# A mamba recurrence on one core: the order of three small matmul pieces around the D groups

## The chip, the cores and the metric

The kernel runs on one core of one Trainium2 chip. The metric is the device time of one execution in microseconds (us); smaller is better. Five engines work side by side, each through its own list of instructions in order, and wait for each other through semaphores: TensorE (PE, matmuls and transposes, into PSUM), VectorE (DVE), ScalarE (ACT), GpSimd (POOL) and SyncE (SP, which here issues the DMA transfers).

## What is computed

The reference chains four layers over an image tensor `x` of 4 x 64 x 128 x 128 in float32: a mamba block (layer 0), a windowed transform with a small block MLP (layer 1), two 3x3 convolutions with a pooled channel gate (layer 2), and a block with two convolutions, a mamba and a feed-forward part (layer 3). The change touches the two mambas only. Cut to what matters, a mamba computes, over tokens `t` of a sequence, with 128 inner channels and N states (16 in layer 0, 64 in layer 3):

```python
xc    = silu(conv4(u @ in_proj_x) + conv_b)        # causal, 4 taps
z     = u @ in_proj_z
dt, Bm, Cm = split(xc @ x_proj_w.T)
delta = softplus(dt @ dt_proj_w.T + dt_proj_b)
def step(h, t):
    h = h * exp(delta[t][:, None] * A) + (delta[t] * xc[t])[:, None] * Bm[t][None, :]
    return h, h @ Cm[t]
y = ys + xc * D
y = y * silu(z)
```

After it come an output projection and a normalization.

## The kernel before

Both mambas are one class, `_Mamba`. The 65536 tokens are cut into 64 chunks of TC = 1024. The recurrence of one chunk is done for 128 x N pairs of channel and state. Four states times 32 channels fill the 128 partitions, so one **group** (four states) takes ND = 4 **iterations**, one for each quarter j of the channels. One iteration is one scan over 1024 tokens on DVE (L593, `tensor_tensor_scan`), written into a ring of eight slots, and one product with C on POOL (L596). A chunk has 4 groups in layer 0 (16 iterations) and 16 in layer 3 (64). An iteration's place in its chunk is called its **position** here.

Groups come in two kinds; layer 0 has "DADA", layer 3 "DADAADAADADAADAA". They differ in how the scan's input, delta * xc * B, comes about:

- **A group**: ScalarE (L387, and one block in eight on POOL, L391) scales the transposed delta * xc by B into `bxT`; PE turns it back, eight 128x128 transposes an iteration (L494), into a PSUM tile `bx`. This PSUM tile is "tile i" of iteration i.
- **D group**: PE spreads B over the partitions once for the group (L500, two matmuls into a `bx` buffer), and DVE multiplies it by the loaded delta * xc in each iteration (L587) into another `bx` buffer.

There are two `bx` buffers. A D group holds both for its four iterations. So the transposes for the first tile of the A group behind it wait for the last L587 of the D group, and those for the second tile wait for the D group's last scan.

The output y of a chunk gathers in one PSUM buffer. `_sums(u, None)` opens it: eight matmuls of xc with a diagonal of D (L410). `_sums(u, h)` adds a group's four products, for half h of the tokens: four matmuls (L413), two and three iterations after the group's last. When a chunk's last group is in, `gated` multiplies y by silu(z) on DVE (L619, called at position 3 of the next chunk), and that frees the PSUM buffer for the next `_sums(u, None)`.

Everything else (projections, convolution, the small matmuls for delta, B and C, the output projection and its norm) is written as generators, called feeds. Each is cut into **pieces**: a few matmuls into the one PSUM buffer `pm`, which then is read by another engine before the next piece can have it. `ahead` makes xc and sz (pieces z and conv), `prepare` the recurrence's inputs (v, C, u, step, B, duT; u is not a piece but one DVE and one POOL instruction), `behind` the output (project, norm). They are put between the iterations in two ways:

- In layer 0 `slots` gives the iteration, counted from the start of the feed's own chunk, at which each piece goes in. With 16 iterations a chunk, -43 is position 5, -37 is 11, -24 is 8, -22 is 10, -21 is 11, -16 is 0, -14 is 2, -7 is 9. The budget there is 12 steps an iteration, more than is ever used.
- In layer 3 there are no slots. A `budget` says how many steps (one or a few matmuls) may go in beside each iteration: in an A group 0, in a D group 2, 2, 2, 1. A feed that waits gives a number of iterations to let pass.

The order of all this is written out by hand in `run`, and `pin` ties it down on every engine. One iteration i issues, in this order: the end of a finished piece; loads of C; the exponentials for the scan three ahead (ACT, L556); the scalings for the next A group; `behind` with `gated`, when a chunk is full; `produced(i + 1)`, which is the next tile's transposes or the next D group's spread; in a D group L587; the scan; the product with C; the state's copy after the fourth; sums that are owed; and, by `beside`, the pieces. `_sums(u, None)` is owed at the iteration of its group's last scan, so before the change it is issued behind that scan.

Of the kernel before, what the change touches and what calls it, by code (L numbers as in the profile page):

```python
# [12 lines left out]
ALU = mybir.AluOpType  # L13
# [5 lines left out]
B, C, HH, WW = 4, 64, 128, 128  # L19
HW = HH * WW  # L20
TC = 1024
NH = TC // 512
# [3 lines left out]
ND = DI // DD  # L26
# [117 lines left out]
class _Mamba:  # L144
# [173 lines left out]
    def prepare(self, c):  # L318
        nc, K, nst, xc = self.nc, self.K, self.nst, c["xc"]

        pos, e, l, u = (self.tmp(k) for k in ("pos", "e", "l", "u"))
# [4 lines left out]
        nc.scalar.activation(e, e, AF.Exp, scale=-1.0)  # L326
        nc.scalar.activation(l, e, AF.Ln, bias=1.0)

        yield self.slot(c, "C")
        r = self.wC.shape[1]  # L330
        pm = yield from self.piece(
# [4 lines left out]
        c["C"] = self.dram.tile([nst, TC], F32, name="c2", tag="c2")  # L336
        for h in range(NH):
            nc.sync.dma_start(c["C"][:, _COLS[h]], cr[r * h : r * h + nst, :512])

        yield self.slot(c, "u")  # L340
        nc.vector.tensor_scalar(u, e, 1.0, 1.0, ALU.add, ALU.subtract)
        nc.gpsimd.tensor_sub(u, e, u)
        yield self.slot(c, "step", 4)
        pm = yield from self.halves((K.eye, pos), (K.eye, l), (K.eye, u))
        nc.scalar.copy(pos, pm)
# [18 lines left out]
        duT = c["duT"] = self.wp.tile([P, NB, DI], F32, name="duT", tag="duT")  # L364
# [56 lines left out]
    def run(self, chunks, ahead, behind, leads, budget):  # L421
# [3 lines left out]
        nc = self.nc  # L425
        its, us = [], []
        for i, c in enumerate(chunks):
            c["no"] = i
            for g, kind in enumerate(self.kinds):
                u = {"c": c, "g": g, "kind": kind, "hc": [], "at": len(its), "last": len(its) + ND - 1}  # L430
# [18 lines left out]
        owed, full = [], None  # L449
# [35 lines left out]
        def produced(i):  # L485

            if i == n:
                return
            v, j = its[i]
            if v["kind"] == "A" or i == v["at"]:  # L490
                bx = bxs[i] = self.bp.tile([P, TC], F32, name="bx", tag="bx", bufs=2)
            if v["kind"] == "A":
                for k in range(NB):
                    nc.tensor.transpose(  # L494
                        bx[:, P * k : P * (k + 1)], v["bxT"][:, k, :, :, j].rearrange("p q e -> p (q e)"), self.K.eye
                    )
            elif i == v["at"]:
                v["B"] = bx
                for k in _COLS:
                    nc.tensor.matmul(bx[:, k], self.spread[v["g"]], v["c"]["xc"][:, k], start=True, stop=True)  # L500
# [25 lines left out]
        at = -1  # L526
        for c in chunks[1:]:
            at = max(at + 1, per * c["no"] - leads[0])
# [3 lines left out]
        for i, (u, j) in enumerate(its):  # L532
# [20 lines left out]
            while nexp < min(n, i + 4) and its[nexp][1] in its[nexp][0]["c"].get("dl", ()):  # L553
                v, k = its[nexp]
# [11 lines left out]
            while credit >= 0.5:  # L566
                if not todo:
# [4 lines left out]
                    v = groups[nmul]  # L572
# [6 lines left out]
            if full and full[0] <= i:  # L579
                started(behind(full[1], self.gated(full[1])), i)  # L580
                full = None
            produced(i + 1)
            if u["kind"] == "D":
                if i == u["at"]:
# [12 lines left out]
            if j == ND - 1:  # L597
                nc.gpsimd.tensor_copy(self.state[:, :, u["g"]], self.ring[:, slot - j : slot + 1, GAP + TC - 1])
            u["hc"].append(hc)
            if i == u["last"]:  # L600
                owed += [(i, u, None)] * (u["g"] == 0) + [(i + 2, u, h) for h in range(NH)]
            while owed and not full and (owed[0][0] <= i or i + 1 == n):
                _, v, h = owed.pop(0)
                self._sums(v, h)
                if v["g"] == self.ng - 1 and h == NH - 1:
                    full = i + 1, v["c"]
# [38 lines left out]
@with_exitstack  # L645
def layer0(ctx, tc, K, w, x, x1):
    nc = tc.nc
    slots = {"z": -43, "conv": -37, "v": -24, "C": -22, "u": -21, "step": -16, "B": -14, "duT": -7}
    slots |= {"project": 22, "rstd": 23, "store": 29}
    m = _Mamba(ctx, tc, K, 16, w, "DADA", {"xc": 3, "sz": 4, "tmp": 5}, slots)  # L650
    cp, wp = m.cp, m.wp
# [626 lines left out]
def layer3_mamba(ctx, tc, K, w, t3, x3, s3, n3):  # L1278

    nc = tc.nc  # L1280
# [74 lines left out]
            nc.sync.dma_start(_halves(n3[b], t0)[h], o[64 * h : 64 * (h + 1)])  # L1355

    chunks = [{"at": (b, t0), "reset": t0 == 0} for b in range(B) for t0 in range(0, HW, TC)]
    m.run(chunks, ahead, behind, (64, 36), [x for k in m.kinds for x in ([2, 2, 2, 1] if k == "D" else [0] * ND)])


@with_exitstack
# [265 lines left out]
```

## Time and profile before

| what | value |
|---|---|
| median of 3 runs | 19720.83 us (19693.8 to 19727.24) |
| profiled execution | 19736.35 us, span of its instructions 19734.5 us |
| mean granted TensorE clock in it | 0.869 |
| layer 0, first to last scan | about 71 to 3665 us |
| layers 1, 2 and the convolutions of 3 | about 3665 to 6226 us |
| layer 3's mamba, first to last scan | 6226 to 18439 us |
| layer 3's feed-forward part | 18439 us to the end |
| L593, the scan | x4848 at 2335 ns and x272 (the first of a sequence) at 2276 ns |
| L587, the product of a D group | x2048 at 1228 ns |
| L596, the product with C on POOL | x5120 at 2378 ns |
| L494, one transpose | x24576, mean 338 ns as recorded |
| L410, the D matmuls | x2048 records (two for each matmul), 592 to 1063 ns |

The page is one profiled execution. Its first part gives each engine's busy time, the second cuts the span into 40 slices and gives the busy share of each engine in tenths. Waits name the engine and line that stood still, and the instruction whose end released it. In the timeline a row is a start, a duration (of the whole row when several instructions are merged), engine, line, operation, output and inputs; what stands in brackets is the idle time of that engine before the row, and who ended it. Matmuls in float32 appear as two records, overlap each other, and their ends are modelled.

### The profile page before, as it was taken

How to read it: one execution, taken by the hardware profiler on the slowest of the kernel's cores; microseconds unless marked ns; L12 is line 12 of the kernel's file. 1: busy time of each engine (PE TensorE's matmuls, PEld its weight loads, DVE VectorE, ACT ScalarE, POOL GpSimd, SP SyncE). 2: the span in 40 equal slices, each digit the busy share in tenths (PEclk: the TensorE clock that was granted, in tenths of full speed). 3: DMA queues.
4: the chain of work that ended last, by engine and by line, in shares of the span. 5: the costliest groups of instructions: out<-in, count | busy, mean ns of one | idle time of the engine just before them, and what ended most of it. 6: DMA issues, size and time to landing. Idle time of an engine off the chain costs nothing. (4 is left out here: it accounts for less than half of the span.)

```text
span 19734.5 us, 238606 instructions
## 1 busy us (share of the span) xinstructions
PE 15294.8 (78%) x80186; PEld 7627.5 (39%) x80186; DVE 15836.0 (80%) x8739; ACT 14933.8 (76%) x30369; POOL 14205.9 (72%) x8094
## 2 busy tenths in 40 slices
PE   7778788778897777777777777777777777777777
PEld 3333333367434333333333333333333333333222
DVE  7888888722124999999999999999999999999755
ACT  7888888411324988889888888988889888888422
POOL 6888888500003898899988989998898988989300
PEclk8999899879998888888888888888888888888888
DMA  5555555300212232332323233232322323233111
GB/s 138 152 150 153 154 150 151 95 37 26 75 56 65 75 88 77 84 82 79 87 75 87 78 83 86 76 88 77 83 82 79 87 76 86 78 82 85 46 43 38
DMA packets 669524, 1722.89 MB, mean 87 GB/s; under 512 B 196785, under 2 KB 231937, under 8 KB 660865
## 3 DMA queue, kind: packets, MB, share of 16 engines
q1 hardware_dynamic: 668288, 1707.62, 31.6%
q8 instruction: 629, 10.31, 0.2%
q14 instruction: 607, 4.96, 0.1%
HBM read 1434.27 MB, written 272.63 MB: 86 GB/s over the span
## 5 line engine op out<-in xcount | busy, mean ns | idle before, releaser
L596 POOL TENSOR_TENSOR ring<-ring,cb 128x1024 f32<-128x1024 f32 x5120 | 12086.1, 2378 | 1653.5 <-DVE ring L593 1340.8
L593 DVE TENSOR_TENSOR_SCAN ring<-da,state,bx 128x1024 f32<-128x1024 f32 x4848 | 11143.4, 2335 | 971.1 <-PE bx L494 697.9
L556 ACT ACTIVATE da<-dl,A 128x1024 f32<-128x1024 f32 x5120 | 5868.2, 1146 | 1383.0 <-DVE ring L593 1365.9
L387 ACT ACTIVATE bxT<-duT,BT 128x128 f32<-128x128 f32 x21504 | 6757.2, 387 | 0.0
L494 PE MATMUL bx<-cst,bxT 128*128 128x128 f32 x24576 | 4458.7, 338 | 2842.8 <-DVE bx L587 2053.0
L494 PEld LDWEIGHTS bx<-cst,bxT 128*128 128x128 f32 x24576 | 3743.1, 214 | 4917.0 <-DVE bx L587 2068.7
L413 PE MATMUL y<-ring,cst 128*32 128x512 f32 x20480 | 3566.6, 660 | 332.4 <-POOL ring L596 332.2
L587 DVE TENSOR_TENSOR bx<-du,bx 128x1024 f32<-128x1024 f32 x2048 | 2515.5, 1228 | 339.6 <-PE bx L500 219.1
L413 PEld LDWEIGHTS y<-ring,cst 128*32 128x32 f32 x20480 | 532.3, 112 | 1735.7 <-POOL ring L596 856.1
L1145 PE MATMUL cv<-img,cw 64*64 64x512 f32 x9216 | 1008.2, 594 | 74.6 <-DMA img<-d_x 45.6
L500 PE MATMUL bx<-xc,spread 128*128 128x512 f32 x2048 | 1018.0, 620 | 1.4
L1427 POOL MEMSET h<- 128x18 f32 x64 | 8.3, 132 | 1180.5 <-PE pd L1489 793.5
L1076 POOL TENSOR_TENSOR xs<-xs,cl 128x1024 f32<-128x1024 f32 x32 | 74.9, 2340 | 1068.4 <-DVE cl L1075 1068.4
L391 POOL TENSOR_TENSOR bxT<-duT,BT 128x512 f32<-128x512 f32 x768 | 809.2, 1054 | 11.5 <-ACT duT L370 11.5
L1310 POOL MEMSET X<- 64x1 f32 x4 | 0.4, 89 | 1122.4 <-DMA cw<-in_l_conv_wT 1122.4
L1489 PE MATMUL pd<-h,diag 64*64 64x512 f32 x4608 | 687.9, 610 | 0.7 <-issue 0.7
L1145 PEld LDWEIGHTS cv<-img,cw 64*64 64x64 f32 x9216 | 437.2, 134 | 643.5 <-issue 568.0
L593 DVE TENSOR_TENSOR_SCAN ring<-da,bx 128x1024 f32<-128x1024 f32 x272 | 609.4, 2276 | 72.4 <-PE bx L494 52.8
L500 PEld LDWEIGHTS bx<-xc,spread 128*128 128x128 f32 x2048 | 347.7, 189 | 687.7 <-issue 464.1
L1461 DVE SCALAR_TENSOR_TENSOR g<-h,dww,g 128x2048 f32<-128x2048 f32 x256 | 602.0, 2352 | 11.2
L1441 ACT ACTIVATE h<-ph,ff_fc_b 128x384 f32<-128x384 f32 (+1 forms) x384 | 200.7, 577 | 497.9 <-PE ph L1436 480.1
L1059 ACT COPY O<-p 128x1024 f32<-128x1024 f32 x32 | 32.4, 1012 | 691.7 <-PE p L1052 691.7
(321 smaller groups left out, 13361.0 us busy)
## 6 DMA issues: line engine op xcount, KB each, us to landing
cb<-c SPq DMA_DIRECT2D x5120, 128.0 KB, 2.8
dl<-d SPq DMA_DIRECT2D x2048, 128.0 KB, 3.4
du<-d SPq DMA_DIRECT2D x2048, 128.0 KB, 3.0
d<-pos SPq DMA_DIRECT2D x128, 512.0 KB, 2.6
d<-u SPq DMA_DIRECT2D x128, 512.0 KB, 3.0
X<-d_t SPq DMA_DIRECT2D x124, 256.0 KB, 4.0
S<-in_x SPq DMA_DIRECT2D x120, 256.5 KB, 4.4
res<-in_x SPq DMA_DIRECT2D x128, 128.0 KB, 3.8
```

Source lines behind the costliest of these rows:

```text
L387: nc.scalar.activation(t[:, k, q].rearrange("p e j -> p (e j)"), c["duT"][:, k, :], AF.Copy, scale=c["BT"][:, k, n : n + 1])
L391: nc.gpsimd.tensor_mul(t[:, k].rearrange("p q e j -> p q (e j)"), c["duT"][:, k].unsqueeze(1).to_broadcast(shape), c["BT"][:, k, NQ * g : ...
L413: nc.tensor.matmul(c["y"][DD * j : DD * (j + 1), _COLS[h]], K.sel, hc[:, _COLS[h]], start=False, stop=u["g"] == self.ng - 1,)
L494: nc.tensor.transpose(bx[:, P * k : P * (k + 1)], v["bxT"][:, k, :, :, j].rearrange("p q e -> p (q e)"), self.K.eye)
L500: nc.tensor.matmul(bx[:, k], self.spread[v["g"]], v["c"]["xc"][:, k], start=True, stop=True)
L556: nc.scalar.activation(das[nexp], v["c"]["dl"][k], AF.Exp, scale=self.A[:, k, v["g"] : v["g"] + 1])
L587: nc.vector.tensor_mul(bxs[i], u["c"]["du"][j], u["B"])
L593: nc.vector.tensor_tensor_scan(hs, das.pop(i), bxs.pop(i), 0.0 if u["c"].get("reset") else st, ALU.mult, ALU.add)
L596: nc.gpsimd.tensor_mul(hc, hs, u["cb"])
L1145: nc.tensor.matmul(p[i][half[h]], W[half[i], k, :], src[half[i], at : at + 4, dx : dx + WW], start=k == 0, stop=k == 8,)
L1461: nc.vector.scalar_tensor_tensor(g1, tap, wk, g1, ALU.mult, ALU.add)
L1489: nc.tensor.matmul(pd[i][half[h]], diag[half[i], k, :], h0[half[i], r : r + 4, dx : dx + WW], start=k == 0, stop=k == 8,)
```

## The change

Four edits, in the two mambas:

1. `_sums(u, None)` of a chunk is owed from the first iteration of its first group, and is issued in the iteration of that group's last scan ahead of `produced(i + 1)`, so ahead of the first transposed tile behind this D group, and ahead of the last L587 and scan, where it stood behind them.
2. In layer 3 the budget beside the last iteration of a D group goes from 1 to 0.
3. In layer 0 the slots change: conv -37 to -38, C -22 to -18, u -21 to -22.
4. u's two instructions stand ahead of piece C in `prepare`, in both mambas.

```diff
@@ prepare
+        yield self.slot(c, "u")
+        nc.vector.tensor_scalar(u, e, 1.0, 1.0, ALU.add, ALU.subtract)
+        nc.gpsimd.tensor_sub(u, e, u)
+
         yield self.slot(c, "C")
...
-        yield self.slot(c, "u")
-        nc.vector.tensor_scalar(u, e, 1.0, 1.0, ALU.add, ALU.subtract)
-        nc.gpsimd.tensor_sub(u, e, u)
         yield self.slot(c, "step", 4)
@@ run
+            if not full and owed and owed[0][2] is None and owed[0][0] <= i:
+                self._sums(*owed.pop(0)[1:])
             produced(i + 1)
...
+            if i == u["at"] and u["g"] == 0:
+                owed.append((u["last"], u, None))
             if i == u["last"]:
-                owed += [(i, u, None)] * (u["g"] == 0) + [(i + 2, u, h) for h in range(NH)]
+                owed += [(i + 2, u, h) for h in range(NH)]
@@ layer0
-    slots = {"z": -43, "conv": -37, "v": -24, "C": -22, "u": -21, "step": -16, "B": -14, "duT": -7}
+    slots = {"z": -43, "conv": -38, "v": -24, "u": -22, "C": -18, "step": -16, "B": -14, "duT": -7}
@@ layer3_mamba
-    m.run(chunks, ahead, behind, (64, 36), [x for k in m.kinds for x in ([2, 2, 2, 1] if k == "D" else [0] * ND)])
+    m.run(chunks, ahead, behind, (64, 36), [x for k in m.kinds for x in ([2, 2, 2, 0] if k == "D" else [0] * ND)])
```

## The prediction

> **What bounds the kernel now.** I read the page first (busy shares, 40 slices), then busy time by stage, then who waits for whom in the two mamba stages, then the timeline of one chunk of each. The page gives the stages: two long plateaus, layer 0 in slices 1 to 7 and layer 3's mamba from slice 13 on, and in both VectorE (DVE) is the fullest engine.
>
> ```profile
> DVE  7888888722124999999999999999999999999755
> ...
> 71.00:3665.00 3594.00, 2858.07 (x13614) 1378.82 (x13614) 3114.90 (x1662) 3108.67 (x5740) 3034.39 (x1657) 0.90 0.57 150
> 6226.00:18439.00 12213.00, 9296.48 (x44194) 4609.74 (x44194) 11361.83 (x5757) 10948.82 (x23391) 10991.09 (x6203) 0.86 0.30 81
> ```
>
> The columns after the length are PE, PEld, DVE, ACT, POOL, then the granted clock. In layer 3's mamba DVE is busy 11361.8 of 12213 us (93%), POOL and ACT 90%. What DVE is not busy is what the change can win; what ends that idle time is mostly one thing, first for layer 3, then for layer 0:
>
> ```profile
> DVE ring L593 <- PE bx L494: 470.2, 423, 3.7
> ...
> DVE ring L593 <- PE bx L494: 280.6, 186, 10.9
> ```
>
> The scan waits for transposed tiles: 470 us in layer 3, 281 us in layer 0. I then took, for every scan (L593) of the trace, its start minus the start of the scan before, and averaged by position in the chunk (64 positions in layer 3, 16 in layer 0). An undisturbed A position takes 2.24 us, a D position 3.71. Layer 3 stands out at position 3 (4.70, the L619 product on DVE itself), 5 (4.04), 13 (4.62), 39 (3.68) and by 0.6 at 19, 31, 36, 47, 59. Layer 0: 5 (4.03), 8 (5.20 for 3.71), 12 (3.21), 13 (4.82). The diff is aimed at positions 5 and 12/13. One chunk of layer 3 shows both; positions 2 to 6 first:
>
> ```profile
> 8144.66 1.20 DVE L619 TENSOR_TENSOR yg<-y,sz 128x1024 f32<-128x1024 f32 x1
> 8145.78 1.22 DVE L587 TENSOR_TENSOR bx<-du,bx 128x1024 f32<-128x1024 f32 x1
> ...
> 8147.05 1.98 PE L494 MATMUL bx<-cst,bxT 128*128 128x128 f32 x8 [5.65 <-DVE bx L587]
> ...
> 8148.97 3.13 PE L410 MATMUL y<-xc,dD 128*32 128x512 f32 x16
> ...
> 8152.02 2.19 PE L494 MATMUL bx<-cst,bxT 128*128 128x128 f32 x16
> ...
> 8153.36 4.59 DVE L593 TENSOR_TENSOR_SCAN ring<-da,state,bx 128x1024 f32<-128x1024 f32 x2 [1.67 <-PE bx L494]
> ```
>
> PE idles until the last D product (L587) frees a PSUM buffer, transposes tile 4, then does the D-times-x sums (L410), and only then tile 5: scan 5 waits 1.67 us. Positions 11 to 14, PE then DVE:
>
> ```profile
> 8172.74 1.98 PE L494 MATMUL bx<-cst,bxT 128*128 128x128 f32 x8 [3.98 <-DVE bx L587]
> 8174.65 1.97 PE L259 MATMUL pm<-tr,cst 128*64 128x512 f32 x2
> 8176.41 1.92 PE L259 MATMUL pm<-yg,woT 128*64 128x512 f32 x2
> 8178.25 2.33 PE L494 MATMUL bx<-cst,bxT 128*128 128x128 f32 x16
> ...
> 8179.73 4.58 DVE L593 TENSOR_TENSOR_SCAN ring<-da,state,bx 128x1024 f32<-128x1024 f32 x2 [2.35 <-PE bx L494]
> ```
>
> Half of the project piece (L259, two matmuls) stands between tiles 12 and 13. The same place of layer 0:
>
> ```profile
> 1252.01 1.05 PE L259 MATMUL pm<-xc,wC 128*32 128x512 f32 x4 [3.39 <-ACT duT L370]
> 1253.00 1.98 PE L494 MATMUL bx<-cst,bxT 128*128 128x128 f32 x8
> 1254.78 4.52 PE L259 MATMUL pm<-S,cw 128*128 128x512 f32 x8
> 1259.13 2.10 PE L494 MATMUL bx<-cst,bxT 128*128 128x128 f32 x16
> ```
>
> [...] eight transposes (L494) take 1.98 us after 3.98 or 5.65 us of idle and 1.1 to 1.24 in a busy stretch; over the whole trace no burst after more than 4.1 us of idle starts fast, and of layer 0's C pieces, which come after 3.39 us, about half do. [...] at 8243 to 8254 us of the trace three groups of transposes with 0.7 to 0.9 us between them stay at 1.72 to 1.98 us, and the sums after them still take 1.94 instead of 1.07. [...]
>
> **The change part by part** (64 chunks in each mamba stage; Y is the end of L619).
>
> *Sums of D times x ahead of tile 4.* They need only L619, since that frees y, so they can start at Y+0.06 instead of Y+3.11 (8148.97 less 8145.86). But tile 4 now comes behind them. Before: scan 4 at Y+3.50, scan 5 at Y+7.50. After, at half clock: the sums end at Y+3.7 (3.64 us is the longest block of 16 in the trace), tile 4 takes another 1.4 to 2.0, scan 4 starts at Y+5.4 and scan 5, 2.26 later, at Y+7.7: the stall has only moved from scan 5 to scan 4, 0.15 us is lost. If the clock comes up after 2.6 us of sums, as it does in most of layer 3's blocks before, they end at Y+3.2, scan 4 is at Y+4.55, and 0.7 is won. PE has idled 4.46 us by then, so it starts at half clock; the full 1.8 us of position 5 is out of reach in layer 3. I take a gain of 0.3 (bounds -0.15 and +0.75): 19 us. In layer 0 PE has idled 3.36 us, about even odds of a fast start; but there PE works without a gap from tile 4 to the spread matmuls that position 8 waits for, and a late scan 4 delays tile 6, which reuses its buffer. A gain appears only if scan 4 starts before Y+4.8: +1.1 with a fast start, -0.6 with a slow one throughout. I take +0.2: 13 us.
>
> *Layer 3, budget 0 beside the last D scan.* The project step leaves position 11 and both steps run at position 20, a D position, where no tile is due until 23 and PE sat idle over 5 us: hidden; without that cover it would cost the 3.8 us of PE once more. Position 13 falls from 4.62 to 2.24: 2.38 won. What is late next: tiles 12 to 14 and the sums of the D group now start on an idle, slow PE without a piece between, as at positions 23 to 27, 35 to 39, 43 to 47 and 55 to 59 today. There the group's fourth scan loses 0, 1.44, 0.60 and 0.68, mean 0.68. Net 1.70 x 64 = 109 us (bounds 0.94 and 2.38: 60 to 152). The other step that moves is half of the B piece, position 43 to 52; position 45 loses 0.07 now: 4 us. u (DVE 0.67, POOL 2.37) goes from beside scan 36 to beside scan 35; position 36 loses 0.6 now, and a D position will instead: 0. Layer 3: 19 + 109 + 4 = 132 us won.
>
> *Layer 0, conv from -37 to -38, C from -22 to -18, u from -21 to -22.* Modulo 16, conv goes from position 11 to 10, C from 10 to 14, u from 11 to 10. At 10 the piece waits, as C does now, for ScalarE's copy of duT to free the one pm buffer (0.05 us after it, 0.26 before scan 11 starts; call this time Q). Before: C, tile 12, conv, tile 13 follow from Q and scan 13 starts at Q + 0.26 + 3.21 + 4.82 = Q+8.29. After: conv, then tiles 12 and 13. Conv's eight records take 3.70 us fast; PE has idled 3.39 us, starts fast about half of the time, but tile 12 in today's order is mostly slow, and the clock is back by about Q+3.2. So conv takes 4.85; scan 12 is at Q + 4.75 + 1.42 = Q+6.17, scan 13 at Q+8.43. The stall moves from 13 to 12 and 0.14 us is lost (bounds: +1.0 at full clock, -0.9 slow throughout): -9 us. S's load leaves SP behind the same conv and ScalarE's two silu passes and table loads follow it; the exponential queued behind them is for scan 14 now, due about 1.2 us after it ends: no cost. u's 0.67 us of DVE falls before scan 11 and is covered by the wait at 12.
> C at 14 goes between the last sums and the spread matmuls for position 0. The spread ends 0.2 us before scan 15 does, C takes 0.95 in a busy stretch: position 0 loses 0.75, 48 us. Its output is wanted by the cb loads 12 positions later: covered. SP waits for cr's copy at 15 instead of 11; no load for the next four scans stands behind it. Layer 0: 13 - 9 - 48 = 44 us lost.
>
> *Sum.* 132 - 44 = 88 us. The profiled execution took 19736.35 us (span 19734.5), so 19648; it lies 15.5 above the median 19720.83, which gives 19633.
>
> **The rivals.**
> 1. *The slow clock decides, and it becomes slower.* Where: conv and the D-times-x sums now open a burst on a PE that has idled 3.4 to 4.5 us, ahead of the tile that DVE waits for. Price if it stays slow through them: layer 0 -0.9 - 0.75 - 0.6 = 2.25 us a chunk, 144 us; layer 3 -0.15 + 0.94 + 0.07 = 0.86, 55 us won. Net 89 us slower, 19810. It decides once layer 0 loses more than layer 3 wins, with layer 3 at its low end once layer 0's loss passes 0.86 a chunk. For it: three of four groups led by transposes stay slow. Against it: today's D-times-x blocks are mostly fast at the end.
> 2. *The clock is kind.* Layer 3 2.38 + 0.75 + 0.07 = 3.2 us a chunk, 205; layer 0 +1.1 + 1.0 - 0.75 = 1.35, 86: 291 us, 19430. Against it: no fast start after such idle times in layer 3.
> 3. *POOL takes over.* It is busy 90% in layer 3; eight A scans cost it 8 x 2.37 + 2 x 1.05 + 0.4 = 21.5 us against 17.9 on DVE. If its lag returns through the sums on PE and eats three quarters of position 13's 109 us, layer 3 keeps 19 + 27 and layer 0's 44 lost cancel it: 19719, no change. Against it: a D group gives POOL 1.3 us back at each position, 5.2 in all, more than the 3.6 that two A groups owe.
> That the reordering doesn't happen I exclude: the instruction order on PE shows L410 ahead of 24 transposes, and conv, tiles 12 to 14 and C at their new places.
>
> **How the numbers follow.** Forecast 0.52, rival 1 0.20, rival 2 0.12, rival 3 0.16. The forecast's own range is 19570 to 19700. Change can be told beyond 0.2% (39 us): below 19681 or above 19760. Faster: 0.46 of the forecast + 0.12 = 0.58; same: 0.06 + 0.13 of rival 3 + 0.02 = 0.21; slower: 0.18 + 0.03 = 0.21. The range 19520 to 19780 leaves out most of rival 2 and the upper half of rival 1, about 2 in 10.
>
> **What would show it.** Right: layer 3's position 13 near 2.24 with 0.3 to 1.4 lost at 15; scan 4 late instead of scan 5 in both layers, with the sum of positions 4 and 5 nearly the 6.3 of before; layer 0's position 11 at 4.4, 12 at 5.2 and 13 at 2.26, position 0 at 4.5. Wrong: positions 4 and 5 both at 2.26 in layer 3 (a clock that I don't expect), conv over 6 us in layer 0, or position 0 unchanged because C found a gap.

## The result, and the profile after

The changed kernel takes 19522.11 us (median of 4 runs, 19521.25 to 19528.66), the kernel before beside it 19722.29 us: the ratio is 0.9902, with a 95% interval of 0.9885 to 0.9919. 200 us were won, where 88 were forecast. The profiled execution took 19528.66 us, its span is 19526.9, and the mean granted TensorE clock rose from 0.869 to 0.882.

VectorE's row of the page's 40 slices, then busy time by stage (layer 0, then layer 3's mamba; columns as in the prediction: length, PE, PEld, DVE, ACT, POOL, granted clock), then what DVE and PE wait for in layer 3's mamba (total, times, longest). The scan is L595 in this kernel.

```profile
DVE  6888888722122999999999999999999999999755
...
69.00:3737.50 3668.50, 2877.46 (x13614) 1371.33 (x13614) 3096.25 (x1661) 3113.36 (x5739) 3011.11 (x1657) 0.91 0.57 147
6302.70:18229.10 11926.40, 9023.87 (x44194) 4573.01 (x44194) 11346.65 (x5757) 10914.56 (x23390) 10988.17 (x6203) 0.87 0.31 83
...
DVE ring L595 <- PE bx L494: 182.4, 269, 4.4
DVE ring L595 <- ACT bxT L387: 57.7, 36, 2.2
DVE ring L595 <- ACT da L556: 27.2, 24, 1.2
...
PE bx L494 <- ACT bxT L387: 23.1, 25, 1.6
```

From first to last scan, layer 0 grew from 3593.4 to 3668.5 us (+75.1; +44 was forecast), and layer 3's mamba shrank from 12213.0 to 11926.4 (-286.6; -132 was forecast). All else is within 4 us of before. Layer 3's scans wait 182 + 58 + 27 = 267 us instead of 470 + 25 = 495. The parts that stand against ScalarE (ACT: 58 + 27 us, and 25 before) are waits for tiles too: all but two of these scans start within 0.15 us of the end of their tile's last transpose, as nearly all of those do that stand against PE. Since DVE's busy time is nearly the same (11347 against 11362 us), the gain is idle time that went.

Start minus start of the scan before, averaged over chunks 2 to 61 as in the prediction, shows where (us a chunk, after minus before). The 16 groups of layer 3 run DADAADAADADAADAA in the kernel, one letter fewer than printed above, so its D positions are 0 to 3, 8 to 11, 20 to 23, 32 to 35, 40 to 43 and 52 to 55.

| place | predicted | measured |
|---|---|---|
| layer 3, positions 4 and 5 (sums) | -0.30 | +1.58 - 1.78 = -0.20 |
| layer 3, 13 (project) | -2.38 | -2.38 |
| layer 3, 15 and 16 (late next) | +0.68 | +0.60 + 0.44 = +1.04 |
| layer 3, 35 and 36 (u), 45 (B) | 0 and -0.07 | +0.40 - 0.58 = -0.18 and -0.08 |
| layer 3, 20 (start of a D group, where project now runs) | 0 | -0.28 |
| layer 3, 19, 27, 31, 32, 39, 40, 47, 51, 59, 63 | 0 | -2.57 |
| layer 0, 4, 5 and 7 (sums) | -0.20 | +1.97 - 1.77 + 0.52 = +0.72 |
| layer 0, 12 and 13 (conv) | +0.14 | +2.61 - 2.56 = +0.05 |
| layer 0, 0 (C) | +0.75 | +0.54 |

At the places that it named in layer 3, the prediction is close, in part by errors that cancel: -1.80 us a chunk, or -2.08 with position 20, times 64 is -115 to -133 us, for -132. The excess is in the row of positions that no edit touches: 2.57 x 64 = 164 us. They are positions 39 (-1.08), 59 (-0.68), 31 (-0.52), 47 (-0.46), 19 (-0.41) and smaller ones, with 27 (+0.35) and 51 (+0.56) against them. At position 20, as at 32 and 40, the first D product of a group (L589, L587 before) waits less for the group's spread matmuls (L500): in all 64 chunks 9.7 us at position 20, for 30.5 before. Of the runs below, those with edit 2 gain 0.19 to 0.35 there, `e4_dose` and `e7_small` 0.10 and 0.12, the others less.

The changed places first. Positions 3 to 5 of one layer 3 chunk, PE then DVE:

```profile
8181.66 3.64 PE L410 MATMUL y<-xc,dD 128*32 128x512 f32 x16 [3.98 <-DVE yg L623]
8185.23 2.99 PE L494 MATMUL bx<-cst,bxT 128*128 128x128 f32 x16
...
8187.35 6.82 DVE L595 TENSOR_TENSOR_SCAN ring<-da,state,bx 128x1024 f32<-128x1024 f32 x3 [2.16 <-ACT bxT L387]
```

The sums start as soon as L623 (the yg product) has freed y, and run 3.64 us, all at half clock, as in 32 of layer 3's 64 chunks (in the others they take 1.92 to 3.28); tiles 4 and 5 follow in one row of 16 transposes. Scan 4 starts 2.16 us after DVE ran dry. The row names ScalarE, whose last scalings ended just before, but PE has worked without a gap since the sums began: the wait is for PE. At this position 73.8 us of such waits stand against ScalarE (47.4 and 26.4 of the two rows above), and all of these scans start 0.13 or 0.14 us after their tile's last transpose. The wait for the transposes moved from scan 5 to scan 4. Positions 11 to 16, DVE then PE:

```profile
8209.02 9.07 DVE L595 TENSOR_TENSOR_SCAN ring<-da,state,bx 128x1024 f32<-128x1024 f32 x4
8218.93 9.19 DVE L595 TENSOR_TENSOR_SCAN ring<-da,state,bx 128x1024 f32<-128x1024 f32 x4 [0.84 <-PE bx L494]
...
8215.57 1.94 PE L413 MATMUL y<-ring,cst 128*32 128x512 f32 x8
8217.43 1.39 PE L494 MATMUL bx<-cst,bxT 128*128 128x128 f32 x8
```

The 2.35 us wait at scan 13 is gone: four scans follow each other without a gap. What is late next is the group's fourth scan, at 15, behind sums of 1.94 us. Position 16 is late too, in 39 of 64 chunks, and there ScalarE does count: PE's own waits for the scalings (23.1 us, 25 times; 2.4 us and 4 times before) all lie at position 16. The likely reason, which no run sets apart: ScalarE does silu's two table loads (1.28 us each in this chunk, at 8206.89 and 8210.35) and two passes (1.11 and 1.14 us) for conv at 10 to 12, and this row of scans now runs earlier by the 2.4 us that scan 13 no longer waits, so the scalings come late. Layer 0, positions 10 to 14, PE then DVE:

```profile
1275.02 5.40 PE L259 MATMUL pm<-S,cw 128*128 128x512 f32 x8 [3.40 <-ACT duT L370]
...
1281.51 9.06 DVE L595 TENSOR_TENSOR_SCAN ring<-da,state,bx 128x1024 f32<-128x1024 f32 x4 [3.33 <-PE bx L494]
```

Conv opens the burst after 3.40 us of idle and takes 5.40 us (the median of its 64 pieces too); scan 12 waits 3.33 us, and the three behind it do not wait.

Now a place that the change leaves alone: positions 56 to 59 of layer 3. The kernel before, PE, then DVE, then two stretches (columns as by stage; the granted clock is the third number from the end):

```profile
8305.94 1.98 PE L494 MATMUL bx<-cst,bxT 128*128 128x128 f32 x8 [0.47 <-DVE ring L593]
8308.18 1.98 PE L494 MATMUL bx<-cst,bxT 128*128 128x128 f32 x8 [0.26 <-DVE ring L593]
8310.09 1.92 PE L413 MATMUL y<-ring,cst 128*32 128x512 f32 x8
8311.94 1.23 PE L494 MATMUL bx<-cst,bxT 128*128 128x128 f32 x8
...
8303.54 9.08 DVE L593 TENSOR_TENSOR_SCAN ring<-da,state,bx 128x1024 f32<-128x1024 f32 x4
8313.28 4.58 DVE L593 TENSOR_TENSOR_SCAN ring<-da,state,bx 128x1024 f32<-128x1024 f32 x2 [0.66 <-PE bx L494]
...
8303.50:8311.80 8.30, 7.57 (x32) 4.93 (x32) 8.26 (x4) 7.57 (x19) 6.95 (x5) 0.50 0.38 114
8311.90:8315.50 3.60, 3.43 (x28) 2.23 (x24) 2.94 (x2) 1.91 (x4) 3.60 (x2) 1.00 1.01 236
```

The changed kernel, the same instructions:

```profile
8337.45 1.98 PE L494 MATMUL bx<-cst,bxT 128*128 128x128 f32 x8 [0.47 <-DVE ring L595]
8339.69 1.66 PE L494 MATMUL bx<-cst,bxT 128*128 128x128 f32 x8 [0.25 <-DVE ring L595]
8341.28 1.07 PE L413 MATMUL y<-ring,cst 128*32 128x512 f32 x8
8342.29 1.23 PE L494 MATMUL bx<-cst,bxT 128*128 128x128 f32 x8
...
8335.05 13.55 DVE L595 TENSOR_TENSOR_SCAN ring<-da,state,bx 128x1024 f32<-128x1024 f32 x6
...
8335.10:8340.80 5.70, 4.98 (x21) 4.18 (x22) 5.70 (x3) 4.97 (x13) 4.36 (x4) 0.50 0.34 96
8340.90:8346.20 5.30, 4.77 (x36) 2.65 (x34) 5.30 (x3) 4.41 (x10) 5.30 (x3) 1.00 0.78 203
```

The order on PE is the same, and so is the start: a slow PE behind a D group. Before, the clock came back 8.3 us after the first scan of the row (8311.87 less 8303.54), so the sums took 1.92 us and the last tile was 0.66 us late. After, it came back 5.8 us after that scan (8340.86 less 8335.05), the sums took 1.07, and six scans run in one row.

Why it comes back at another time can be read from the clock records of the two traces: in each, the granted clock changes only at multiples of one window of 3413.33 ns (to 0.6 ns from the first record to the last), and in each window it is half or full.

In these traces the clock of a window goes with how busy PE was in the window before. This is worked out from the traces of before and after, over the windows between the first and the last scan in which PE did some transposes and nothing else; busy is the share of the window in which a matmul is recorded as running. At half clock, none of the 683 windows under 82% was followed by full clock, and all 120 with 88% or more were. At full clock, none of the 214 under 52% was followed by full clock, and 329 of the 335 with 54% or more were. Between these borders it went both ways. Over windows with matmuls of every kind they are less sharp: of those at half clock, 10 of 1044 under 80% and 1136 of 1193 with 88% or more were followed by full clock. The two cuts above show it. Before, the window from 8305.04 to 8308.46 us holds 0.43, 1.98 and 0.28 us of transposes, 79%, and the clock stays at half for one more window. After, the window from 8337.45 to 8340.86 holds 1.98 and 1.17 us, 92%, and the next one is at full clock. The tiles are the same and so are the pauses between them; they lie elsewhere in the windows. So here the same burst of PE work got another clock because it fell at another place in the windows. The distances of chunk starts, in windows (64 chunks, 63 distances), worked out from the scans' starts:

```
                  layer 3: most frequent distances           mean us
before            56.0 in 41 of 63, 56.1 in 10               190.94
after             54.4 in 18, 54.6 in 16, 54.8 in 7          186.41
```

Before, nearly every chunk lasts 56.0 windows (191.15 us), so each meets the clock in the same phase as the one before, and each waits at the same places: scans 19, 31, 47 and 59 wait for transposes in 60, 59, 55 and 59 of the 64 chunks. After, the two most frequent lengths are 185.7 and 186.3 us, often in turn, and 28 of the 62 pairs of neighbours last 109.0 windows (to 0.1) together; the same four scans wait in 17, 10, 27 and none of the chunks. The half clock's share of layer 3 fell from 0.284 to 0.250.

Scan 59 shows across kernels that this phase, the place of a chunk's work in the windows, sets the wait. In nine runs (before, after and those experiments below that add no zero matmuls) the order on PE from tile 56 to tile 59 is the same. Of their 576 chunks, scan 59 waits in all 161 in which the transposes of tile 56 start 1.4 to 2.4 us after the edge of a window, and in none of the other 415. Before, 59 of 64 chunks start there; after, none. In the same runs scans 15, 19, 31, 39, 47 and 59 wait 1396 times, and in only one of these cases was the clock full, but for 2% at most, from the start of the tile before to the end of their own. Scans 16 and 51 are different: there 103 of 134 and 198 of 396 waits came at full clock.

### The profile page after: what moved, and what is told of

Read it like the earlier page. It is cut to its first block, busy times and chain, and to the rows that moved or that the text cites. A ratio compares the mean times of both kernels' runs of the same rounds, so it can differ in the third digit from the quotient of the medians.

```text
span 19526.9 us, 238778 instructions
## 1 busy us (share of the span) xinstructions
PE 15043.2 (77%) x80186; PEld 7722.0 (40%) x80186; DVE 15802.2 (81%) x8739; ACT 14903.7 (76%) x30369; POOL 14180.5 (73%) x8094
## 5 line engine op out<-in xcount | busy, mean ns | idle before, releaser
L595 DVE TENSOR_TENSOR_SCAN ring<-da,state,bx 128x1024 f32<-128x1024 f32 x4848 | 11122.1, 2335 | 804.3 <-PE bx L494 352.6
L413 PE MATMUL y<-ring,cst 128*32 128x512 f32 x20480 | 3459.6, 638 | 379.1 <-POOL ring L598 378.7
L589 DVE TENSOR_TENSOR bx<-du,bx 128x1024 f32<-128x1024 f32 x2048 | 2514.6, 1228 | 336.2 <-PE bx L500 211.6
L500 PE MATMUL bx<-xc,spread 128*128 128x512 f32 x2048 | 1017.0, 619 | 3.7 <-DVE ring L595 1.6
L1149 PEld LDWEIGHTS cv<-img,cw 64*64 64x64 f32 x9216 | 576.4, 134 | 507.2 <-issue 369.3
L410 PE MATMUL y<-xc,dD 128*32 128x512 f32 x2048 | 428.5, 983 | 438.7 <-DVE yg L623 438.7
L259 PE MATMUL pm<-S,cw 128*128 128x512 f32 x1024 | 577.0, 704 | 188.3 <-ACT duT L370 172.1
L595 DVE TENSOR_TENSOR_SCAN ring<-da,bx 128x1024 f32<-128x1024 f32 x272 | 608.1, 2275 | 62.7 <-PE bx L494 45.4
L500 PEld LDWEIGHTS bx<-xc,spread 128*128 128x128 f32 x2048 | 347.7, 189 | 691.0 <-issue 407.6
```

The source lines that it names most:

```text
L413: nc.tensor.matmul(c["y"][DD * j : DD * (j + 1), _COLS[h]], K.sel, hc[:, _COLS[h]], start=False, stop=u["g"] == self.ng - 1,)
L589: nc.vector.tensor_mul(bxs[i], u["c"]["du"][j], u["B"])
L595: nc.vector.tensor_tensor_scan(hs, das.pop(i), bxs.pop(i), 0.0 if u["c"].get("reset") else st, ALU.mult, ALU.add)
L1149: nc.tensor.matmul(p[i][half[h]], W[half[i], k, :], src[half[i], at : at + 4, dx : dx + WW], start=k == 0, stop=k == 8,)
```

## The experiments

Two readings were set against each other. In the first (theory A in the expectations), every edit acts where it stands and the edits add up. In the second (theory B), the waits at the untouched places hang on the phase between the chunk and the clock's windows, and whatever disturbs that phase moves them. Times without a range are of one run, with before at 19725 us beside them. Places are given as in the table above, in us a chunk against before.

### One edit at a time

`e1_budget`: the budget alone in layer 3, the sums alone in layer 0.

```diff
+            if not full and owed and owed[0][2] is None and owed[0][0] <= i and self.ng == 4:
+                self._sums(*owed.pop(0)[1:])
             produced(i + 1)
...
-    m.run(chunks, ahead, behind, (64, 36), [x for k in m.kinds for x in ([2, 2, 2, 1] if k == "D" else [0] * ND)])
+    m.run(chunks, ahead, behind, (64, 36), [x for k in m.kinds for x in ([2, 2, 2, 0] if k == "D" else [0] * ND)])
```

> The kernel before with two single edits in separate stages: in layer 3 only the budget 2, 2, 2, 0; in layer 0 only the D-times-x sums ahead of tile 4. Theory A (every edit acts at its own place, places add up): layer 3 changes at positions 13 (-2.4 us) and 15/16 (+0.7 to +1.0) and by no more than 0.1 anywhere else, so a chunk goes from the typical 191.15 us to about 189.6, 90 to 110 us in all; layer 0 changes at 4 (+2.0), 5 (-1.8) and 7 (+0.5), +45 us in all. Theory B (the chunk of layer 3 locks to the clock gate's windows of 3.413 us, 56.00 of them before and 109 for two chunks after the change): positions that the edit doesn't touch (19, 31, 39, 47, 59) change by 0.3 us or more too, and the usual chunk is a multiple of half a window: 189.4, 187.7 or 186.0.

Measured: 19553.47 us. Layer 3 -227.9 us: position 13 -2.38, 15 +0.23, 16 +0.84, and -0.61 at 19, -0.58 at 31, -0.37 at 39, -0.30 at 59. Layer 0 +43.5: position 4 +1.70, 5 -1.77, 7 +0.55. The own-place sum of layer 3 (-1.31 x 64 = -84 us) is far too small. In layer 0 the sums alone lose 43.5 us.

`e2_sums`: the sums alone in layer 3, C at -18 alone in layer 0.

```diff
+            if not full and owed and owed[0][2] is None and owed[0][0] <= i and self.ng != 4:
+                self._sums(*owed.pop(0)[1:])
             produced(i + 1)
...
-    slots = {"z": -43, "conv": -37, "v": -24, "C": -22, "u": -21, "step": -16, "B": -14, "duT": -7}
+    slots = {"z": -43, "conv": -37, "v": -24, "C": -18, "u": -21, "step": -16, "B": -14, "duT": -7}
```

> The kernel before with the D-times-x sums ahead of tile 4 in layer 3 only, and in layer 0 only C's slot from -22 to -18 (conv stays at -37, u at -21). Theory A: layer 3 changes at 4 (+1.6) and 5 (-1.8) only, 10 to 15 us faster in all. Theory B: layer 3's usual chunk is still 56 windows, 191.15 us, and what 4 and 5 give is taken at other positions, or the chunk leaves 56 windows altogether and 19, 31, 39, 47, 59 change. Layer 0 under both: 12 falls by about 1 us since C no longer stands ahead of tile 12, 13 falls with it or keeps its wait for conv, 0 rises by 0.5.

Measured: 19730.59 us. Layer 3 -129.5 us, although positions 4 and 5 give only +1.58 - 1.78; the rest is 39 (-0.90), 47 (-0.48), 59 (-0.45), with 51 (+0.58). Layer 0 +118 us: position 0 +0.75, as predicted for C, but 13 +1.77: tile 12 and conv now come straight after PE's idle time, where C had come first, and conv takes 6.08 us at the median, for 3.88 before.

`e3_slots`: u ahead of C alone in layer 3, the three slots without the sums in layer 0.

```diff
+        yield self.slot(c, "u")
+        nc.vector.tensor_scalar(u, e, 1.0, 1.0, ALU.add, ALU.subtract)
+        nc.gpsimd.tensor_sub(u, e, u)
         yield self.slot(c, "C")
...
-    slots = {"z": -43, "conv": -37, "v": -24, "C": -22, "u": -21, "step": -16, "B": -14, "duT": -7}
+    slots = {"z": -43, "conv": -38, "v": -24, "u": -22, "C": -18, "step": -16, "B": -14, "duT": -7}
```

> The kernel before with u ahead of C (both stages), which is all that changes in layer 3, and in layer 0 the three new slots without the new place of the sums. Theory A: layer 3 changes at 35 (+0.4) and 36 (-0.6) only, about 10 us faster; layer 0 at 12 (+2.6), 13 (-2.6) and 0 (+0.5), 35 us slower. Theory B: layer 3's chunk stays at 56 windows and the 0.2 us of 35/36 come back elsewhere; layer 0's sum differs from 35 us by more than 20.

Measured: 19568.53 us. Moving two small instructions of DVE and POOL by one position gives layer 3 -204.7 us: +0.39 - 0.58 at 35 and 36, and -1.34 at 39, -0.68 at 59, -0.61 at 47, -0.55 at 5, with 45 (+0.74) against them. 32 of 63 chunks last 55.0 windows, another 24 are within 0.1 of it, so the 56 windows that theory B expected did not hold either. Layer 0 +19 us.

The three edits of layer 3, each alone, win 227.9 + 129.5 + 204.7 = 562 us; together they win 287. They do not add up. In layer 0 they nearly do: 43.5 + 19 = 62.5, against 75.1 together.

### Work added, nothing moved

`e4_dose`: before, with a DVE copy of a tile onto itself ahead of one scan a chunk, at position 21 in layer 3 and 9 in layer 0.

```diff
+            for _ in range(1 * (i % per == {4: 9, 16: 21}[self.ng])):
+                nc.vector.tensor_copy(das[i], das[i])
             nc.vector.tensor_tensor_scan(
```

> The kernel before with one more DVE instruction a chunk (a copy of 128 x 1024 onto itself, between 0.6 and 1.2 us) ahead of the scan at position 21 of layer 3 and 9 of layer 0. All of it lies on the DVE path between two D scans. Theory A: every chunk becomes longer by the length of the copy: 64 times that in each stage. Theory B: layer 3's chunk stays at 56.00 windows, 191.15 us, and the copy disappears in waits that shrink elsewhere, so that layer 3 becomes longer by less than a third of it; layer 0, whose chunks were not locked to one length before, becomes longer by something else than the sum.

The 0.6 to 1.2 us are an estimate; in the trace of before, DVE's TENSOR_SCALAR on 128 x 1024 takes 694 ns (L1075) or 765 (L341), its product 1228 (L587).

Measured: 19766.52 us. One copy takes 1882 ns at the median (686 at least, 4498 at most). Position 21 grows by 2.08 us, 133 us in all, but layer 3 by only 4.5: -0.80 at 39, -0.67 at 59, -0.63 at 31, -0.59 at 47, with +0.90 at 51 and +0.63 at 27. Save 27 and 51, these are places that gain in the changed kernel. In layer 0 position 9 grows by 1.72 us, 110 us in all, and the layer by 26: 12 (-0.93) and 13 (-0.34) give most of it back. Only 13 chunks of layer 3 last 56.0 windows, so theory B had the sum right and the fixed length wrong.

`e7_small` and `e12_tiny` were to shift the phase at nearly no cost: before, with a DVE operation on 128 columns in place of 1024 at position 21 of layer 3, first a copy, then the maximum of a tile with itself.

```diff
+            if self.ng != 4 and i % per == 21:
+                nc.vector.tensor_copy(das[i][:, :128], das[i][:, :128])
...
+                nc.vector.tensor_tensor(das[i][:, :128], das[i][:, :128], das[i][:, :128], ALU.max)
             nc.vector.tensor_tensor_scan(
```

> The kernel before with a short DVE copy (128 x 128, some 0.1 to 0.5 us) ahead of the scan at position 21 of layer 3 only. Theory A: every chunk of layer 3 becomes longer by the length of that copy. Theory B: if the lock to 56.00 windows has slack, the usual chunk is still 191.15 us and layer 3 is not longer; if it has none, the chunk leaves 56.00 and, as in e3_slots, may become shorter by 1 to 3.5 us though work was added.

> The kernel before with a DVE maximum of a 128 x 128 tile with itself (0.1 to 0.5 us, on the DVE path) ahead of the scan at position 21 of layer 3. Places add up: layer 3 longer by 64 times its length. Lock with slack: the usual chunk stays at 56.00 windows, 191.15 us, and layer 3 is not longer by more than 5 us, waits elsewhere (19, 31, 39, 47 or 59) being shorter by the length of the instruction.

The 0.1 to 0.5 us are an estimate; in the trace of before, DVE's copies of 128 x 128 outside this loop take 218 to 292 ns (L201, L880, L941, L211), its TENSOR_TENSOR of that size 281 to 292.

Measured: 19727.15 us for the copy. For the maximum, 19735.26 us (12 runs, 19727.78 to 19749.44), ratio 1.001 (1.0001 to 1.0019). The small operations were not small. The copy (minimum, median and maximum of one, in ns):

```profile
L594 DVE COPY da<-da x64: 1401/1416/4102, 6296.2 to 18306.3; 128x128 f32<-128x128 f32 x64
```

The maximum takes 1477 ns at the median (1461 at least, 4075 at most). Their ends go with POOL's in the traces: all 64 copies end 81 to 89 ns, and all 64 maxima 145 to 153 ns, after the end of an operation of POOL, in most cases the one that was running when they began.

They cost 1.67 and 1.52 us a chunk at position 21, 107 and 97 us, and layer 3 was no longer for it (13.7 and 6 us shorter, less than the 48 us by which runs of before differ), through the same untouched places. So they failed as a pure shift: only 19 and 29 of 63 chunks stay within 0.1 of 56.0 windows. They do show again that added time is paid for by waits that go elsewhere: about 100 us put on the path of the fullest engine cost about 14 us (19735.26 less 19721.59, the medians; the interval reaches from 2 to 37).

### The clock itself

`e5_mix` joins layer 0 of before with layer 3 of after, to see whether the stages act on each other. In layer 0 u's old place behind C is restored too, which the cut leaves out.

```diff
-            if not full and owed and owed[0][2] is None and owed[0][0] <= i:
+            if not full and owed and owed[0][2] is None and owed[0][0] <= i and self.ng != 4:
...
-    slots = {"z": -43, "conv": -38, "v": -24, "u": -22, "C": -18, "step": -16, "B": -14, "duT": -7}
+    slots = {"z": -43, "conv": -37, "v": -24, "C": -22, "u": -21, "step": -16, "B": -14, "duT": -7}
```

> Layer 0 as in the kernel before, layer 3 as in the kernel after. Both theories: the stages are apart, so layer 0 takes 3593 us as before and layer 3 11926 us as after, 75 us less than the kernel after, about 19450. A difference of more than 30 us from that would say that layer 3's length depends on how it is entered.

Measured: 19469.07 us, layer 0 3596.7, layer 3 11929.2. The stages are independent here: each takes, within 4 us, what it took in the kernel that it comes from.

`e6_warm` and `e8_warmb` keep PE from idling: four matmuls with zero weights add nothing to y in the third iteration of each D group but a chunk's first in layer 3, in `e6_warm` on top of `e5_mix`, in `e8_warmb` on top of before.

```diff
+        self.zero = cp.tile([P, DD], F32, name="zero")
+        nc.vector.memset(self.zero, 0.0)
...
             beside(i, budget[i % per])
+            if u["kind"] == "D" and u["g"] and j == 2 and self.ng != 4:
+                for k in _COLS[:1]:
+                    for jj in range(ND):
+                        nc.tensor.matmul(u["c"]["y"][DD * jj : DD * (jj + 1), k], self.zero, u["hc"][1][:, k], start=False, stop=False)
```

> As e5_mix, and in layer 3, in each D group but the first of a chunk, four more matmuls with zero weights behind the third scan, added to the open y sums (they add zero). They wait for the product of the second scan and so fall into PE's idle time ahead of the next tile. Theory B (the stalls at 15, 16, 27, 39, 51 are the half clock after idle time): these positions fall to 2.3 us or less, 2 us and more a chunk, and layer 3 comes to about 11790 us. Rival (they come from the order on PE, sums ahead of tiles, at any clock): they stay within 0.1 us each, and layer 3 stays at 11926 or becomes longer by the 1 to 2 us that the extra matmuls take where they stand in the way.

> The kernel before with the same extra matmuls as e6_warm in layer 3. Theory B: 19, 31, 39, 47 and 59 fall to 2.3 or less, while the waits that stand in the order of the matmuls stay: 5 at about 4.0 and 13 at 4.2 to 4.6. A chunk falls from 191.15 to about 187.5 us, and the distance to e6_warm is what the edits bring at their own places, 2.5 to 2.9 us a chunk, 160 to 185 us. Rival: as for e6_warm.

Measured: `e6_warm` 19428.6 us, layer 3 11888.6, 41 us less than in `e5_mix`, where about 140 were expected. The half clock's share fell from 0.252 to 0.187, yet 15 (2.77), 16 (2.76) and 51 (3.01) stay late. At 16 the releaser is ScalarE; at positions 15 and 16, PE then DVE:

```profile
8147.61 0.99 PE L502 MATMUL bx<-cst,bxT 128*128 128x128 f32 x6
8149.80 1.47 PE L502 MATMUL bx<-cst,bxT 128*128 128x128 f32 x10 [1.21 <-ACT bxT L395]
...
8150.44 4.59 DVE L603 TENSOR_TENSOR_SCAN ring<-da,state,bx 128x1024 f32<-128x1024 f32 x2 [0.96 <-PE bx L502]
```

PE is not at half clock (0.99 us for six transposes; eight take 1.98 at half), and the wait is the scalings': PE waits for them at position 16 in 32 chunks, 28.5 us. At 51 the clock falls to half at 8243.06 us, behind a window in which PE did nothing but transposes for 44% of the time. By the shares given above this is too little (none of 214 windows under 52%). A scan takes 2.24 us and its tile 1.23 at full clock, so a row of tiles alone fills 55%, which is close to the 52 to 54% counted above.

`e8_warmb` took 19532.2 us: layer 3 -215.7 us with the order of before, nothing of the change in it. Positions 11 to 14, PE then DVE:

```profile
8151.01 1.23 PE L496 MATMUL bx<-cst,bxT 128*128 128x128 f32 x8 [1.41 <-DVE bx L589]
8152.17 1.07 PE L261 MATMUL pm<-tr,cst 128*64 128x512 f32 x2
8153.07 1.02 PE L261 MATMUL pm<-yg,woT 128*64 128x512 f32 x2
8154.03 1.23 PE L496 MATMUL bx<-cst,bxT 128*128 128x128 f32 x8
...
8151.05 9.06 DVE L595 TENSOR_TENSOR_SCAN ring<-da,state,bx 128x1024 f32<-128x1024 f32 x4
```

The project piece still stands between the two tiles, but its matmuls take 1.07 and 1.02 us instead of the 1.97 and 1.92 of before, and position 13 falls from 4.62 to 2.53. The expectation had been that 13 would stay at 4.2 to 4.6. So most of the wait that edit 2 removes was the half clock: at full clock the piece leaves only a small part of it. Positions 31, 39, 47 and 59 lose 0.59 to 0.82 here too; 43 of 63 chunks last 55.0 windows. Against them stand 16 (+0.89), 51 (+0.88) and 19 (+0.26), which did not fall as expected. At 16 PE waits for ScalarE's scalings in 56 chunks, 81.6 us in all.

### Filling more, and the best of both

`e9_fill0` adds more zero matmuls to `e6_warm`: in layer 3 also in every group's last iteration and every A group's first; in layer 0 ahead of C at position 10, and in piece B one matmul (two records) into the half of `pm` that nothing reads. `e10_fill1` is the same on top of after. `e11_best` is `e9_fill0` without the further ones in layer 3.

```diff
+            if self.ng == 4 and u["g"] == 2 and j == 2:
+                self.fill(u, u["hc"][1][:, :512])
             beside(i, budget[i % per])
...
+            if self.ng != 4 and i + 1 < n and "y" in u["c"] and (j == 3 or j == 0 and u["kind"] == "A"):
+                self.fill(u, u["c"]["xc"][:, :512])
...
-        pm = yield from self.piece(block[: NB // 2], block[NB // 2 :])
+        more = [(lambda pm: pm[:, 512:], K.eye, xc[:, :512], True, True)] if self.slots else []
+        pm = yield from self.piece(block[: NB // 2], block[NB // 2 :] + more)
```

> e6_warm's layer 3 with four more zero matmuls beside the last iteration of every group and the first of every A group (where only transposes run on PE for three tiles in a row), and the order of the kernel before in layer 0 with extra matmuls too: four ahead of C at position 10 (behind the product of scan 9), two behind piece B at position 2. Theory B (the half clock makes the stalls[...]): layer 3's positions 27, 31, 39, 47 and 51 come within 0.15 us of 2.24, 1 us and more less a chunk than e6_warm; 15 or 16 keeps about 0.5, since tile 16 waits there for ScalarE's scaling. Layer 0 at full clock: 5 falls from 4.03 to about 2.3, 13 from 4.82 by about 1 us, 2 to 3 us a chunk in all, so about 19200 us. Rival (order, not clock): layer 0 and layer 3 as in e6_warm or slower by what the extra matmuls take, 19430 to 19550.

> The kernel after (all four edits in both stages) with the same extra matmuls as e9_fill0. Layer 3 as in e9_fill0. Theory B: the loss of 1.27 us a chunk that the edits made in layer 0 was the half clock at positions 3 to 5 and 10 to 12; at full clock 4 and 5 are both about 2.3 and 12 falls from 5.81 to about 4.6, so that only C's 0.5 us at position 0 is left, and layer 0 lies within 40 us of e9_fill0's. Rival: the loss is in the order itself, and layer 0 stays 60 us or more behind e9_fill0's.

> e6_warm's layer 3 (extra zero matmuls behind the third scan of a D group only) with e9_fill0's layer 0. The stages are apart: layer 3 11889 us, layer 0 3520 us, so about 19345. If layer 3 comes out more than 40 us from 11889, its length depends on how its first chunks meet the clock's windows.

| kernel | median us (range) | ratio to before (95%) | layer 0 | layer 3 |
|---|---|---|---|---|
| `e9_fill0` | 19460.55 (19457.19 to 19464.51) | 0.9865 (0.9850 to 0.9879) | 3520.0 | 11998.8 |
| `e10_fill1` | 19511.03 (19509.86 to 19517.9) | 0.9890 (0.9873 to 0.9906) | 3579.5 | 12003.6 |
| `e11_best` | 19328.28 (19327.26 to 19345.59) | 0.9801 (0.9786 to 0.9815) | 3520.1 | 11872.6 |

In layer 3 more filling fails, against the expectation of 1 us and more a chunk. `e9_fill0` brings the half clock down to 0.124 and still is 110 us slower there than `e6_warm`: its matmuls stand in front of tiles (16 takes 3.35; 17, 25 and 57 grow by 0.50 to 0.83 over `e6_warm`). So the clock is not the only thing to pay for.

In layer 0 the filling wins 73 us with the order of before (5 -0.37, 12 -0.53, 13 -0.28; half clock 0.203 to 0.090). With the order of after it wins 89 (3668.5 less 3579.5) but stays 59.5 us behind. What remains there is +0.50 at 0 and +0.51 at 7, so most of layer 0's loss lies in the order, not in the clock.

`e11_best` beats both kernels, after by 194 us. In its two mamba stages PE executes 638 and 2562 more matmul records than in the changed kernel, and the clock is 0.95 and 0.91 for 0.91 and 0.87.

## Why the prediction was right and wrong

The direction was right, and the time lies at the lower edge of the range; the gain was 2.3 times the forecast one. The two stages were wrong in opposite ways: layer 3 won 155 us more than forecast, layer 0 lost 31 more.

**The step that failed is "Layer 3: 19 + 109 + 4 = 132 us won".** It sums three edits at their own places and leaves all other positions at their durations of before. The prediction had taken "0, 1.44, 0.60 and 0.68, mean 0.68" for properties of these places, and even used them as the price of what is late next. The runs showed that they belong to the phase of the clock (scan 59 above): each edit alone, work added without any edit (`e4_dose`, `e7_small`, `e12_tiny`) and zero matmuls (`e8_warmb`) all shorten positions 39, 47 and 59, by 0.16 to 1.34 us. In the changed kernel such untouched places give 164 us, which covers the 155 us (286.6 less 132) that were missing.

That the chunk of before was held at 56.0 windows is read off its durations, in which 41 of 63 agree, and off the same waits in every chunk. No run set the phase alone, so the lock itself is inferred. One thing fits it: within the stretch in which scan 59 waits, a later start means a shorter wait (0.87 us at the near end, 0.42 at the far one), which would draw the chunks to one phase. Left open is why a single edit lets the chunk fall to 55 windows of all lengths, and why the mean stays near 191 us with work added although most chunks leave 56.0.

**Three groups of transposes that "stay at 1.72 to 1.98 us", 8243 to 8254 us:** PE was busy for only 78% and 75% of the two windows of half clock there, too little by the shares worked out above (none of 683 windows under 82%). In the changed kernel, a window that holds transposes alone, 92% busy, is followed by full clock at 8340.86 us.

**Project out of the way, "2.38 won":** exact at position 13. `e8_warmb` adds that 2.09 of it could be had by the clock alone. The price of the next late scan was taken as 0.68 and measured 1.04: 0.60 at 15, and 0.44 at 16, where 25 of the 39 waits come with PE's wait for ScalarE, which the prediction did not foresee.

**Sums ahead of tile 4, layer 3, "a gain of 0.3":** 0.20. The stall moved from scan 5 to scan 4 as described; the block ran slow throughout in half of the chunks, which is between the two cases that the text weighs. That PE "starts at half clock" held in 34 of the 64 chunks; in the other 30 the block started at full clock, after 3.8 to 4.4 us of idle.

**Sums ahead of tile 4, layer 0, "I take +0.2":** 43.5 us lost alone (`e1_budget`), for 13 won. The text had named what decides it (scan 4 before Y+4.8, a late scan 4 delays tile 6) and then took a gain. The sums ran slow throughout in 46 of 64 chunks, where even odds of a fast start were taken. Position 4 came to 4.23, and the unbroken row on PE from tile 6 over z to tile 7 gave 0.52 away at position 7. This is 56 us of an own-place size that was wrong.

**Layer 0's slots, "0.14 us is lost" and "position 0 loses 0.75, 48 us":** together 57 us lost forecast, 19 measured (`e3_slots`). In the changed kernel conv took 5.40 at the median for 4.85, but 12 and 13 together lost only 0.05, and position 0 lost 0.54.

**Rivals.** The first, the slow clock, was right about its mechanism (the sums at half clock for 3.64 us, conv slower than taken) but not about the sign of the whole. The second, a kind clock, was right that far more could be won, but put it at the edited places. Positions 4 and 5 did not become fast, and 164 us came elsewhere. The third, POOL taking over, did not happen: position 13 kept its whole 2.38, though PE's waits for POOL in layer 3's sums grew from 322 to 370 us. What came up behind was ScalarE, by the 23.1 us that PE waits for it at position 16.

## What to carry to other kernels

A periodic loop that starves TensorE at fixed places should be checked for its period in clock windows before the effect of an edit is summed: if chunk after chunk lasts the same whole number of windows (here 56.0 of 3413.33 ns, in 41 of 63 distances), its waits can be properties of the phase, as here, where each edit and each piece of added work redistributed them. Then measure edits together and not one by one, and read the gain at the places that weren't touched as well. A few matmuls that add zero, in the one gap where nothing stands behind them, can be worth nearly as much as a new order (`e8_warmb` won 216 us in layer 3, the change 287), but not in front of a tile that is waited for (`e9_fill0`, in layer 3 110 us slower than `e6_warm`).

A releaser that the profile names is a candidate and no more: 73.8 us of waits at position 4 stood against ScalarE, and the end of the tile on PE, 0.14 us before the scan's start, showed whose they were.

## What the runs showed of the hardware that was not expected

- In the traces the granted clock was a series of whole windows of 3413.33 ns at half or full, and in some versions a loop of 190 us settled on whole or half multiples of them (56.0 before; 55.0 in `e3_slots` and `e8_warmb`; 109 for two chunks in part of after; 16.0 for layer 0's chunk in 45 of 63 cases of `e11_best`). In others it did not: layer 3 of `e11_best` has 54.1 in 19 of 63 and otherwise many lengths.
- Transposes alone brought the clock up and held it, in the traces of before and after. Windows with nothing else were followed by full clock in all 120 cases with PE at least 88% busy at half clock, and in 329 of 335 with at least 54% at full clock.
- About 100 us added to the path of the fullest engine cost 0.1% (`e12_tiny`, ratio 1.001), and two small instructions moved by one position won 205 us of a stage (`e3_slots`).
- A DVE copy of 128 x 128 elements took 1416 ns at the median in this loop (minimum 1401), and one of eight times its size took 686 ns at best and 1882 at the median. So the length of a DVE copy in this loop says little about its size. All 64 small copies, and 126 of the 128 large ones, ended a fixed time (81 to 89 and 547 to 557 ns) after the end of an operation of POOL. That most of their length is a wait for POOL is inferred from this; no run shows why.
